# A chunk of scans waits for its own delta, B and C, and the parts of all images form one stream

## The chip, the cores and the metric

The kernel runs on one core of a Trainium2 chip. The metric is the device time of one execution in microseconds. Before the change three runs took 23043.62, 23055.54 and 23061.29 us; the median, 23055.54 us, is what the change is measured against.

A core has five engines that take their instructions in order, each from its own queue: TensorE (PE, with its weight loads shown as PEld), VectorE (DVE), ScalarE (ACT), GpSimd (POOL) and SyncE (SP), which here issues nearly all DMA transfers. They wait for each other through semaphores.

## The reference, cut to what matters

Eight images of 56 x 56 tokens and 192 channels go through four residual layers, each behind a group norm. The last layer is a selective state-space scan in four directions over the tokens:

```python
x = x + _L0_conv_ref(_gn(x), ...)   # gate over two Toeplitz products
x = x + _L1_conv_ref(_gn(x), ...)   # attention in shifted windows
x = x + _L2_conv_ref(_gn(x), ...)   # depthwise 3 x 3
x = x + _L3_conv_ref(_gn(x), ...)   # selective scan

def _selective_scan(u, delta, A, Bm, Cm, Dp, delta_bias):
    delta = jax.nn.softplus(delta + delta_bias[None, :, :, None])
    dA = jnp.exp(delta[:, :, :, None, :] * A[None, :, :, :, None])
    dBu = (delta * u)[:, :, :, None, :] * Bm[:, :, None, :, :]
    ...
    _, hs = jax.lax.associative_scan(comb, (dA, dBu), axis=-1)
    y = jnp.einsum('bkdnl,bknl->bkdl', hs, Cm)
    return y + Dp[None, :, :, None] * u
```

Here the scan has 384 channels (3 blocks of 128 partitions), 16 states a channel, 3136 tokens and 4 directions, for each of 8 images. `delta`, `Bm` and `Cm` come from the same image's tokens through small matrix products. All is fp32.

## The kernel before, in words

The first part computes the products q*v and the Toeplitz products of all images and leaves them in device memory. What follows concerns the rest, which works image by image.

**The front of an image** is a generator, `front(b)`: `gate`, `attention`, `conv2`, `inner`, `steps`, one after the other. They pass their results through device memory, and all carve their working space out of one SBUF tile, `slab`. A generator yields between small pieces of work, and tells at each yield how many PSUM banks it holds and needs, and whether a load must first land. `steps(b)` is the last stage and makes what the scans read. It has 14 parts, over `o` (0 for the row-wise directions, 1 for the column-wise ones) and `j` (seven chunks of 448 tokens). Each part makes B and C of its chunk (a product on PE, a copy at L853, a store to `bc_d`) and the deltas of two directions (products at L861, bias on ACT at L866, one softplus on ACT at L870 between two loads of function tables, two stores to `dl_d` at L873). All stores and loads here are issued on SP.

**The scans** go over 224 chunks (8 images x 4 directions, called slots, x 7 chunks), in each of which there are 24 "pairs" (3 channel blocks `d` x 8 pairs of states `k`), 5376 pairs in all, 672 an image. A pair is: inject on POOL (delta*u times B, L991), decay on ACT (two exponentials, L1006), one scan on DVE (L1015), the product with C (L1021, on POOL for three of eight `k`, on DVE for the others), the copy of the state for the next chunk (L1028, ACT), and adding up over the states on PE (L1036). Slots 0 and 1 read the `o` = 0 part of `steps`, slots 2 and 3 the `o` = 1 part. A chunk's delta is loaded by `load_delta`, its u by `load_xc`, B and C by `load_bc`, all one chunk ahead.

**The finish** of an image, `finish(b, j)`, normalises and projects one of seven chunks of the summed result. It runs during slot 0 of the next image.

**The order of the work** is made when the program is built. A loop over the pairs emits the scan's instructions, and after each pair calls `parts.step(limits)`. The clients of `parts` are generators, the front of the next image and the current `finish`. `step` goes through them, first those that hold a PSUM bank, and resumes one as long as a small model of each engine's due times says that its piece fits within the limits. Two loops call `step` with the limits `anything`, which means that whatever is left is emitted at once: one before the first chunk of the next image, until its front is done, and two before `ending`, the current `finish`, is wanted done. Since each engine works in the order of emission, everything so forced stands ahead of the next pairs of scans.

The front of image `b + 1` is added at the first pair of image `b`. The loop that forces it stands in the last chunk of image `b`, at (d, k) = (1, 0), which is the 16th pair from the end of the image:

```python
if i + 1 in range(4 * NCH, len(chunks), 4 * NCH):
    while fronts[b + 1] in parts.clients:
        parts.step(anything)
load_delta(i + 1)
```

For image 0 the front runs alone, ahead of the scans. In the last image no front runs.

Of the kernel before, what the change touches and what calls it, by code (L numbers as in the profile page):

```python
# [28 lines left out]
NCH = L // CH  # L29
# [52 lines left out]
def model(ctx: ExitStack, tc: tile.TileContext, a: dict, out: bass.AP):  # L82
    nc = tc.nc
    B = out.shape[0]
# [195 lines left out]
    with (  # L280
# [42 lines left out]
        def bank():  # L323
            return ps.tile([128, 512], F32, name="ps_f")
# [35 lines left out]


        meter, costs = Meter(tc.nc), {}


        st = wp.tile([CP, 2, NCH, 6], F32, name="gn_st")
# [466 lines left out]
        def steps(b):  # L832

            w_x, xc, rc, dl = carve(slab, 128, (2, ND, 128), (2, ND, CH), (2, CH), (2, ND, CH))
            nc.sync.dma_start(out=w_x, in_=a["w_x"])
            todo = [(o, j) for o in range(2) for j in range(NCH)]

            def load_x(n):
                o, j = todo[n]
                nc.sync.dma_start(out=xc[:, n % 2], in_=xc_d[o][b][:, :, j * CH : (j + 1) * CH])  # L840

            load_x(0)
            yield 0, 0, 8.0
            for n, (o, j) in enumerate(todo):
                tok = slice(j * CH, (j + 1) * CH)
                if n + 1 < len(todo):
                    load_x(n + 1)
                yield 0, 1
                p = bank()
                for d in range(ND):  # L850
                    nc.tensor.matmul(p[:, :CH], w_x[:, o, d, :], xc[:, n % 2, d, :], start=d == 0, stop=d == ND - 1)
                yield 1, 0
                nc.scalar.copy(rc[:, n % 2, :], p[:, :CH])  # L853
                nc.sync.dma_start(out=bc_d[o][b][:, tok], in_=rc[64:, n % 2, :])
                for d in range(ND):
                    yield 0, 2
                    held = []
                    for s in range(2):
                        row = slice(32 * s, 32 * s + R)
                        held.append(bank())  # L860
                        nc.tensor.matmul(  # L861
                            held[s][:, :CH], w_dt[row, o, d * 128 : (d + 1) * 128], rc[row, n % 2, :], start=True, stop=True
                        )
                    yield 2, 0
                    for s in range(2):
                        nc.scalar.activation(  # L866
                            dl[:, s, d, :], held[s][:, :CH], AF.Identity, bias=dt_b[:, 2 * o + s, d : d + 1]
                        )
                yield 0, 0
                nc.scalar.activation(dl, dl, AF.Softplus)  # L870
                usual_functions()
                for s in range(2):
                    nc.sync.dma_start(out=dl_d[2 * o + s][b][:, :, tok], in_=dl[:, s])  # L873
            yield 0, 0

        def front(b):
            yield from gate(b)
            yield from attention(b)
            yield from conv2(b)
            yield from inner(b)  # L880
            yield from steps(b)
# [171 lines left out]
        class Parts:  # L1053
# [36 lines left out]
                entry.held, entry.needs, *load = got  # L1090
                entry.ready = at + sum(load)

            def step(self, limit):
                old = [e for e in self.clients if e.held]
                for entry in old + [e for e in self.clients if e not in old]:
                    while entry in self.clients:
                        if entry.held and entry not in old:
                            break
                        if entry.needs + sum(e.held for e in self.clients if e is not entry) > 2:
                            break  # L1100
                        if not self.fits(entry, limit):
                            entry.waits += 1
                            break
                        entry.waits = 0
                        if entry in old:
                            old.remove(entry)
                        self.resume(entry)
# [27 lines left out]
        with tc.manual_schedule():  # L1135
            for k in range(NP):
                load_bc(0, k)
            load_delta(0)
            for d in range(ND):
                xcs[0, d] = load_xc(0, d)  # L1140
                times_x(0, d)
            ahead, last = 2, len(pairs) - 1
            parts = Parts()
            run = parts.run

            fed, set_, scanned, taken, summed = ([0.0] * (len(pairs) + ahead + 8) for _ in range(5))

            def feed(g):
                inject(g)
                fed[g] = run("P", 2.09, taken[g - 5] if g > 4 else 0.0)  # L1150

            def take(g):
                times_c(g)
                after = scanned[g], summed[g - 4] if g > 3 else 0.0
                taken[g] = run("P", 2.0, *after) if on_pool(*pairs[g][1:]) else run("D", 1.09, *after)

            def prepare(g):
                decay(g)
                set_[g] = run("A", 1.3, taken[g - 2] if not on_pool(*pairs[g - 2][1:]) else scanned[g - 2])

            for g in range(ahead):
                feed(g)
            initial(0), initial(1)
            prepare(0)
            fronts = {}
            ending, anything = None, dict.fromkeys("ADE", 1e9)
            for g, (i, d, k) in enumerate(pairs):
                b, slot, j = chunks[i]
                if i % (4 * NCH) == 0 and d == 0 and k == 0 and b + 1 < B:
                    fronts[b + 1] = parts.add(front(b + 1), "front")  # L1170
                more = i + 1 < len(chunks)
                if more and d == 1 and k == 0:
                    if i + 1 in range(4 * NCH, len(chunks), 4 * NCH):
                        while fronts[b + 1] in parts.clients:
                            parts.step(anything)
                    load_delta(i + 1)
                    for e in range(ND):
                        xcs[i + 1, e] = load_xc(i + 1, e)
                if more and (d, k) in ((1, 6), (1, 7), (2, 0)):
                    times_x(i + 1, d + k - 7 if d == 1 else 2)  # L1180
                    run("P", 1.08)
                pi, pd, pk = pairs[g - 1]
                if g + ahead <= last:
                    feed(g + ahead)
                if g and on_pool(pd, pk):
                    take(g - 1)
                if g:
                    keep_state(g - 1)
                    run("A", 0.15, scanned[g - 1])
                if g < last:  # L1190
                    prepare(g + 1)
                if g + 2 <= last:
                    initial(g + 2)
                    run("A", 0.12, taken[g - 3] if g > 2 else 0.0)
                scan(g)
                scanned[g] = run("D", 2.02, set_[g], fed[g])
                if not on_pool(d, k):
                    take(g)
                if g and pd == ND - 1 and pi + 1 < len(chunks):
                    load_bc(pi + 1, pk)  # L1200
                done = (i, d - 1) if d else (i - 1, ND - 1)
                if k == 2 and g > NP and chunks[done[0]][1] == 0:
                    xds[done] = load_xc(*done)
                if slot == 0 and b > 0 and (d, k) == (1, 4):
                    while ending.at < 3:
                        parts.step(anything)
                if k == 4 and g > NP:
                    sums(*done)
                if slot == 0 and b > 0 and ((j, d, k) == (0, 0, 5) or j + 1 < NCH and (d, k) == (2, 4)):
                    while ending in parts.clients:  # L1210
                        parts.step(anything)
                    ending = parts.add(finish(b - 1, j + (d == 2)), "finish")

                n1 = max(parts.t["D"], fed[g + 1], set_[g + 1])
                n2 = n1 + (2.02 if on_pool(*pairs[min(g + 1, last)][1:]) else 3.11)
                parts.step({"A": max(n2, fed[g + 2]) - 0.7, "E": n1 + 5.0, "D": 0.2})
                if g >= 2:
                    add_up(g - 2)
                    summed[g - 2] = run("E", 1.1, taken[g - 2])
            if on_pool(d, k):  # L1220
                times_c(last)
            for g in (last - 1, last):
                add_up(g)
            sums(i, d)
            for j in range(NCH):
                drain(finish(B - 1, j))
# [101 lines left out]
```

## Time and profile before

| | |
|---|---|
| median of three runs | 23055.54 us |
| profiled execution, as timed | 23085.27 us |
| its span, first to last instruction | 23083.3 us |
| mean granted TensorE clock | 0.887 |
| PE busy | 18554.5 us, 80% |
| DVE busy | 16579.4 us, 72% |
| POOL busy | 16157.3 us, 70% |
| ACT busy | 12534.0 us, 54% |
| first scan to end of the last | 3727.4 to 22874.9 us |

The shares are means over stretches of different kinds. The first 3.7 ms are the products, the Toeplitz part and the front of image 0. Then come eight images of scans, each about 2330 to 2490 us from its first scan to the next image's, the last one 2014 us. All scans together are 5376; a scan takes 2.02 us on DVE, an inject 2.10 us and a product with C 2.02 us on POOL, 1.09 us on DVE.

The profile has several views: a page with busy tenths in 40 slices, the waits (who waited for whom, the total, how often, the longest), the timeline of an engine, and busy times by stretch. In a stretch's line stand its bounds and length, for each engine its busy time and in brackets the number of its instructions, then the granted clock, the DMA share and the rate in GB/s.

### The profile page before, as it was taken

The numbers are of one execution on the slowest core, as the hardware profiler recorded it, in microseconds if no ns is written. First come the engines' busy times: TensorE is split into PE (matmuls) and PEld (weight loads), VectorE is DVE, ScalarE is ACT, GpSimd is POOL, SyncE is SP. The second block draws the span as 40 slices with busy tenths as digits, with TensorE's granted clock in tenths as the row PEclk, the third lists the DMA queues.
The fourth block names the chain that finished last, engine by engine and source line by source line (L and its number), as shares of the span: only waits on it lengthen the run. The fifth ranks groups of instructions, "written<-read, shape, count | busy, mean of one in ns | idle before, by whom it ended". The sixth has DMA issues, their size and how long they took to land. (4 is left out here: it accounts for less than half of the span.)

```text
span 23083.3 us, 201064 instructions
## 1 busy us (share of the span) xinstructions
PE 18554.5 (80%) x58660; PEld 9730.9 (42%) x58660; DVE 16579.4 (72%) x13156; ACT 12534.0 (54%) x31864; POOL 16157.3 (70%) x8500
## 2 busy tenths in 40 slices
PE   8866678888887878888888888887888798887666
PEld 4566334434443435343543444343434353333323
DVE  3211114997789768986899778976898689877996
ACT  3211225655666565756565566656664657565554
POOL 0000004987789768976898778877897689778997
PEclk9987778999899989998999889998999899988888
DMA  3488225445544455345544454345534553454332
GB/s 89 109 196 178 67 62 171 135 123 168 167 135 131 142 169 146 124 135 172 151 134 129 161 162 137 122 147 177 148 115 146 168 157 119 140 172 139 126 122 89
DMA packets 2536339, 3220.44 MB, mean 140 GB/s; under 512 B 1045261, under 2 KB 2488687, under 8 KB 2504272
## 3 DMA queue, kind: packets, MB, share of 16 engines
q1 hardware_dynamic: 2515010, 3091.32, 45.2%
q0 software_dynamic: 15520, 116.14, 1.3%
q8 instruction: 465, 7.62, 0.1%
q14 instruction: 640, 5.24, 0.1%
q10 hardware_dynamic: 4704, 0.12, 0.0%
HBM read 2631.56 MB, written 575.48 MB: 139 GB/s over the span
## 5 line engine op out<-in xcount | busy, mean ns | idle before, releaser
L991 POOL TENSOR_TENSOR hs<-du,bm 128x896 f32<-128x896 f32 x5376 | 11124.4, 2102 | 110.1 <-DVE ps_a L1015 90.2
L1036 PE MATMUL ps_y<-hc,ident_sb 128*128 128x448 f32 x21504 | 9913.8, 597 | 947.8 <-POOL hc L1021 846.4
L1015 DVE TENSOR_TENSOR_SCAN ps_a<-ps_a,hs 128x898 f32<-128x898 f32 x3360 | 6793.9, 2022 | 1048.5 <-ACT ps_a L1006 871.5
L1006 ACT ACTIVATE ps_a<-delta,A_logs_sb 128x449 f32<-128x449 f32 x10752 | 6859.4, 638 | 322.2 <-DVE hs L1015 35.9
L1036 PEld LDWEIGHTS ps_y<-hc,ident_sb 128*128 128x128 f32 x21504 | 4339.0, 210 | 5095.4 <-issue 3594.3
L1021 POOL TENSOR_TENSOR hc<-hs,cm 128x896 f32<-128x896 f32 x2016 | 4067.0, 2017 | 2757.2 <-DVE hs L1015 1574.0
L1015 DVE TENSOR_TENSOR_SCAN hs<-ps_a,hs 128x898 f32<-128x898 f32 x2016 | 4064.5, 2016 | 810.3 <-ACT ps_a L1006 779.3
L1021 DVE TENSOR_TENSOR hc<-ps_a,cm 128x896 f32<-128x896 f32 x3360 | 3668.9, 1092 | 1166.1 <-PE ps_y L1036 883.2
L1028 ACT COPY state<-ps_a 128x2 f32<-128x2 f32 x3359 | 528.6, 157 | 4109.0 <-DVE hc L1021 4106.4
L979 POOL TENSOR_TENSOR du<-delta,xcd 128x448 f32<-128x448 f32 x672 | 716.0, 1066 | 1266.1 <-DMA xcd<-xc 1266.1
L263 PE MATMUL ps_tz<-tzx,tm 112*112 112x112 f32 x4608 | 889.3, 369 | 463.5 <-issue 294.7
L802 PE MATMUL ps_f<-slab 128*128 128x448 f32 x2646 | 1096.9, 551 | 85.0 <-DMA slab<-dg_d 58.0
L277 POOL DMA_DIRECT2D o<-tzx x192 | 97.8, 513 | 1490.9 <-DVE tzx L269 1340.1
L263 PEld LDWEIGHTS ps_tz<-tzx,tm 112*112 112x112 f32 x4608 | 883.8, 199 | 469.2 <-issue 468.1
L269 DVE COPY tzx<-ps_tz 112x448 f32<-112x448 f32 x288 | 179.9, 625 | 1172.3 <-PE ps_tz L263 862.0
L996 ACT COPY hs<-state 128x2 f32<-128x2 f32 x4608 | 817.5, 177 | 2.7 <-POOL hc L1021 2.6
L76 PE MATMUL ps_f<-slab 96*96 96x448 f32 (+6 forms) x2306 | 745.3, 519 | 76.1 <-DMA slab<-x 37.4
L269 ACT COPY tzx<-ps_tz 112x448 f32<-112x448 f32 x288 | 153.2, 532 | 1198.1 <-PE ps_tz L263 1067.2
L632 PE MATMUL ps_f<-ident_sb,slab 98*98 98x98 f32 x1344 | 337.9, 322 | 576.3 <-ACT slab L625 576.3
L734 PE MATMUL ps_f<-slab 96*96 96x448 f32 x1764 | 728.9, 549 | 46.4 <-DVE slab L721 46.4
L802 PEld LDWEIGHTS ps_f<-slab 128*128 128x128 f32 x2646 | 509.4, 193 | 598.0 <-issue 528.7
L861 PE MATMUL ps_f<-slab,w_dt_sb 12*128 12x448 f32 x1176 | 507.5, 787 | 309.8 <-ACT slab L853 234.9
(215 smaller groups left out, 17788.8 us busy)
## 6 DMA issues: line engine op xcount, KB each, us to landing
bm<-bc SPq DMA_DIRECT2D x1792, 448.0 KB
cm<-bc SPq DMA_DIRECT2D x1792, 448.0 KB
xcd<-xc SPq DMA_DIRECT2D x840, 224.0 KB
dl<-slab SPq DMA_DIRECT2D x224, 672.0 KB
delta<-dl SPq DMA_DIRECT2D x224, 672.0 KB
tzx<-qv SPq DMA_DIRECT2D x192, 588.0 KB
o<-tzx POOLq DMA_DIRECT2D x192, 588.0 KB, 16.3
slab<-x SPq DMA_DIRECT2D x224, 336.0 KB
```

The costliest lines, as they stand in the source:

```text
L76: return f(*args, **kw)
L263: nc.tensor.matmul(po[:, c, :], t[:, c2 + c, :], x[:, :, c1 + c2 + c], start=True, stop=True)
L734: nc.tensor.matmul(p[:CP, :CH], dg[:, k, t, :], xp[:, u, k, dy : dy + 8, dx : dx + W], start=t == 0, stop=t == 8,)
L802: nc.tensor.matmul(p[:, :CH], dg[:, t, :], xp[:, 8 * j + dy : 8 * j + dy + 8, dx : dx + W], start=t == 0, stop=t == 8,)
L979: nc.gpsimd.tensor_mul(du[:, 0, :], deltas[i][:, d, 1 : CH + 1], xcs.pop((i, d)))
L991: nc.gpsimd.tensor_mul(hs[:, :, tokens(i)[0]], dus[i, d].to_broadcast([128, NG, CH]), bms[i, k])
L996: nc.scalar.copy(hss[g][:, :, tokens(i)[1]], src)
L1006: nc.scalar.activation(dA[:, n, :], deltas[i][:, d, at : at + CH + 1], AF.Exp, scale=negA[:, slot, d, c : c + 1])
L1015: nc.vector.tensor_tensor_scan(h, dA, hs, 0.0, ALU.mult, ALU.add)
L1021: (nc.gpsimd if on_pool(d, k) else nc.vector).tensor_mul(hc, h[:, :, tokens(i)[0]], cms[i, k])
L1028: nc.scalar.copy(states[i][:, d, NG * k : NG * k + NG], h[:, :, tokens(i)[2]])
L1036: nc.tensor.matmul(yps[i, d][:, :CH], ident, hcs[g][:, n, :], start=k + n == 0, stop=k + n == NP + NG - 2)
```

## The change

A set `made` now holds which parts (b, o, j) of `steps` have been emitted. Before a chunk's delta is loaded, the loop forces the front only until that chunk's own part is in the set; this test is made ahead of every chunk, not at the first chunk of an image alone. The front of the next image that has none is added as soon as the former one has ended, even if the scans of the current image are not yet at their start or are in their middle; there is at most one front at a time. `step` gets an argument `only`: when a client is to be forced, the others are resumed only while they hold a PSUM bank. All three forcing loops use it. No operation, no transfer and no buffer is added or taken away; the order of emission changes.

```diff
         meter, costs = Meter(tc.nc), {}
+        made = set()
...
                 for s in range(2):
                     nc.sync.dma_start(out=dl_d[2 * o + s][b][:, :, tok], in_=dl[:, s])
+                made.add((b, o, j))
             yield 0, 0
...
-            def step(self, limit):
+            def step(self, limit, only=None):
                 old = [e for e in self.clients if e.held]
                 for entry in old + [e for e in self.clients if e not in old]:
+                    if only is not None and entry is not only and not entry.held:
+                        continue
                     while entry in self.clients:
...
-            fronts = {}
+            ahead_of, b_next = None, 1
             ending, anything = None, dict.fromkeys("ADE", 1e9)
             for g, (i, d, k) in enumerate(pairs):
                 b, slot, j = chunks[i]
-                if i % (4 * NCH) == 0 and d == 0 and k == 0 and b + 1 < B:
-                    fronts[b + 1] = parts.add(front(b + 1), "front")
+                if ahead_of not in parts.clients and b_next < B:
+                    ahead_of = parts.add(front(b_next), "front")
+                    b_next += 1
                 more = i + 1 < len(chunks)
                 if more and d == 1 and k == 0:
-                    if i + 1 in range(4 * NCH, len(chunks), 4 * NCH):
-                        while fronts[b + 1] in parts.clients:
-                            parts.step(anything)
+                    b1, slot1, j1 = chunks[i + 1]
+                    while (b1, slot1 // 2, j1) not in made:
+                        parts.step(anything, ahead_of)
                     load_delta(i + 1)
...
                 if slot == 0 and b > 0 and (d, k) == (1, 4):
                     while ending.at < 3:
-                        parts.step(anything)
+                        parts.step(anything, ending)
...
                     while ending in parts.clients:
-                        parts.step(anything)
+                        parts.step(anything, ending)
                     ending = parts.add(finish(b - 1, j + (d == 2)), "finish")
```

## The prediction

> **What bounds the kernel now.** I read the page first: its slices, then the groups of the scan. The chain of waits that ended last covers the final image alone and says nothing of the places that the change touches, so after the page I went to the waits of all engines, to the boundaries in time, and to the rate of the scan by stage.
>
> ```profile
> DVE  3211114997789768986899778976898689877996
> POOL 0000004987789768976898778877897689778997
> ```
>
> The scans begin in the seventh slice (first scan at 3727 us) and end at 22875 us. In this stretch no engine is full, except POOL in the last image, where no front runs beside the scans. So the stretch is a mixture, and I look for what stops the scans:
>
> ```profile
> POOL hc L1021 <- DVE hs L1015: 1574.0, 513, 82.4
> DVE ps_a L1015 <- ACT ps_a L1006: 871.5, 295, 344.4
> DVE hs L1015 <- ACT ps_a L1006: 779.3, 106, 81.0
> ```
>
> Columns: total us, times, longest. The longest waits (some 80 us) are out of all proportion to a scan of 2.02 us. The timeline of VectorE and of ScalarE at one of them, at the end of the fourth image (the bracket is idle time and what ended it):
>
> ```profile
> 13361.48 2.04 DVE L1015 TENSOR_TENSOR_SCAN ps_a<-ps_a,hs 128x898 f32<-128x898 f32 x1 [3.37 <-ACT ps_a L1006]
> 13363.62 1.09 DVE L1021 TENSOR_TENSOR hc<-ps_a,cm 128x896 f32<-128x896 f32 x1
> 13439.82 2.03 DVE L1015 TENSOR_TENSOR_SCAN hs<-ps_a,hs 128x898 f32<-128x898 f32 x1 [75.11 <-ACT ps_a L1006]
> ```
> ```profile
> 13434.46 2.44 ACT L870 ACTIVATE slab<-slab 128x2688 f32<-128x2688 f32 x1
> 13436.92 1.28 ACT L321 ACT_TABLE_LOAD   x1
> 13438.21 0.16 ACT L1028 COPY state<-ps_a 128x2 f32<-128x2 f32 x1
> 13438.41 1.31 ACT L1006 ACTIVATE ps_a<-delta,A_logs_sb 128x449 f32<-128x449 f32 x2
> ```
>
> The scan waits for its decay factors (L1006), which stand on ScalarE behind the rest of `steps` of the next image: the planner's loop emitted all of it there. All engines, in three of the seven such stretches, and the sum over all seven (busy us and instructions of PE, PEld, DVE, ACT, POOL, then clock and DMA):
>
> ```profile
> 5959.80:6017.30 57.50, 44.59 (x76) 15.98 (x74) 1.13 (x2) 36.49 (x42) 3.24 (x2) 0.64 0.33 114
> 8421.30:8503.40 82.10, 61.12 (x96) 21.77 (x96) 1.09 (x1) 49.41 (x57) 1.84 (x1) 0.63 0.39 132
> 13363.60:13439.80 76.20, 61.41 (x92) 22.03 (x92) 1.09 (x1) 46.25 (x54) 0.00 (x0) 0.58 0.37 126
> ...
> sum 520.50, PE 408.49 PEld 146.16 DVE 7.68 ACT 316.92 POOL 5.07; mean PE 58.36 PEld 20.88 DVE 1.10 ACT 45.27 POOL 0.72
> ```
>
> POOL, the fullest engine of the scans, does 5 us of work in 520 us. Last, scans per stretch (busy us of L1015 and its count). Fourth image: gate with `finish` beside it, free `steps`, the forced stretch, the tail. Then the first image's gate, without `finish`; then the last image, without a front, its first 153 pairs with `finish`, the rest without:
>
> ```profile
> 11013.00:11554.00 541.00, 279.96 (x139) 0.95 0.55 152
> ...
> 13148.00:13361.00 213.00, 118.48 (x59) 0.83 0.58 204
> 13361.00:13439.00 78.00, 2.04 (x1) 0.58 0.38 130
> 13439.00:13481.00 42.00, 29.94 (x15) 0.85 0.49 160
> ```
> ```profile
> 3730.00:4161.00 431.00, 261.50 (x130) 0.96 0.58 161
> ```
> ```profile
> 20861.00:21369.00 508.00, 307.37 (x153) 0.86 0.43 139
> 21369.00:22872.00 1503.00, 1038.95 (x518) 0.86 0.37 122
> ```
>
> Length over count is the price of a pair: gate and finish 541/139 = 3.89 us, steps 213/59 = 3.61, tail 42/15 = 2.80, gate alone 431/130 = 3.32, finish alone 508/153 = 3.32, nothing beside 1503/518 = 2.90.
>
> **What the Trainium skill says.** "TensorE: Matmul & The Clock Gate", specification table, gives ScalarE, VectorE and GpSimdE a strict first-in first-out queue. The trace agrees: L1006 starts 0.2 us behind the last `steps` instruction, though its inputs had long been there. "ScalarE: Activation LUTs", section "What ACT_TABLE_LOAD costs", says that each load of a table takes about 1283 ns; the trace has 1.28 us, two for each part of `steps`, forced or not, so the change saves none of them. Part 1 of the first page says that an idle PE is clocked down; the granted clock of 0.58 to 0.64 in the forced stretches agrees, and there PE sets no pace.
>
> **The change part by part.** Counts are from the order in which both programs are built; it holds no times. A pair is one scan.
>
> Removed: in before, the last parts of `steps` are forced at pair 656 of each image: 303 of 7 x 128 pieces (a piece runs from one yield to the next), some 45 per image. The scan-to-scan times there are 59.5, 84.2, 78.3, 78.3, 78.3, 78.4 and 78.1 us, 535 in all. Seven ordinary pairs at 3.1 would be 22: gross gain 513 us.
>
> Given back: the same pieces now run beside scans. In before 83 free pieces took 59 pairs, so 45 need some 32. In the built order the front covers the tails (16 pairs of each image) and then runs on into the next: `steps` ends 4, 16, 32, 44, 58, 67 and 67 pairs past the image's end, the next gate begins one pair later. So 110 tail pairs go from 2.80 to 3.61: +89. The lag only shifts later fronts until the last image, where 63 pairs that had only `finish` beside them get `steps` too. This sum, `steps` with `finish`, occurs nowhere in the trace. Adding the surcharge of `finish` (3.32 - 2.90 = 0.42) to 3.61 gives 4.03, so 63 x 0.71 = +45. In the earlier images `steps` takes the gate's place beside `finish`, and the gate comes out at the other end: by the same adding this cancels, since the gate falls from 3.89 to 3.32 outside `finish`. Together +134.
>
> The unknown is thus the price of 260 pairs with both. Lower bound 3.61 (finish hides wholly behind what steps waits for): 260 x 0.42 = 109 better. Upper bound: a surcharge of 1.0, the dearest that the trace has (by the starts of the scans, attention's 81 pairs beside finish take 4.17 us, its others 3.14; the change of stage is in it): 260 x 0.58 = 150 worse. I take 0.42, because the surcharge seen with the gate (0.57, a start of 13 us in 139 pairs among it) is near it.
>
> Still forced: the built order has 7 pieces of the sixth `steps` and, at the seventh, 9 pieces of the end of `inner` and 11 of `steps`, since a lag of 67 pairs leaves the first part too late. A forced piece costs 76.2/45 = 1.7 us: 27 x 1.7 = +46. Bounds: 20 (part of it hidden by scans already fed) and 90 (the seventh crosses from `inner` to `steps`, whose first load must land; that crossing shows scan-to-scan times of 10 to 13 us in the free case).
>
> Gate right behind `steps`: w_p, w_o, x and the o blocks now stand on SP behind the last two delta stores; the first o block overlays those deltas in the slab and must wait for the landing. In the forced stretch a ScalarE instruction waited for such a store until some 5 us after its issue (issued from 13405.89 to 13407.09, the wait over at 13412.07). Behind on SP stand bm, cm, delta and xcd of the next chunk, wanted 5 or more pairs (15 us) later: cost 0, at worst 5 us x 6. The absorb at L396 waited 10 us for w_p before (59.4 us in six) and will again; if w_p comes 5 us later, 30 more. I take 0, with 0 to 60 for the range.
>
> The delta, B and C loads behind the new wait: where the part is made in good time, the store is tens of pairs old and nothing waits. The two waits for `ending` alone: `finish` ends before its boundary in every image of before and is forced for 3 pieces in after, so nothing.
>
> Sum: -513 + 134 + 46 = -333 us on a span of 23083 us, to 22750. The profiled run took 23085.3, 30 us above the median of 23055.5. So 22722 us is the forecast against the median, 1.4% faster.
>
> **The rivals.** Crowding: `finish`, `steps` and two scans' decay contend on ScalarE and PE at the image's start, the 260 pairs cost the upper bound, and the clock, 0.83 in the steps stretch, falls further now that PE has no pause. For it: PE is 79% busy in that stretch (167.9 of 213 us). Against: the planner counts ScalarE and PE before it lets a piece in. Then -333 + 150 + 30 = -153: 22900.
>
> More gain: `finish` hides behind `steps`, and the forced pieces cost little: -333 - 109 - 20 = -462: 22594.
>
> Slower: the handover on SP. The gate's loads stand in front of the B and C loads, wait for landing delta stores, and POOL's inject (in order, L991) starves, and all scans behind it. It decides from 333/7 = 48 us per handover on; at 80 us it is +227: 23280. Against: 5 us is what a landing costs, a tenth of that.
>
> No effect: the stall comes back as forced pieces. The order shows 27 for 303, so this would need the trace to price them ten times dearer: about 23055.
>
> **How the numbers follow.** Chances: forecast 0.74, crowding 0.12, more gain 0.07, no effect 0.03, slower 0.04. The range must hold 0.8: the forecast's own bounds (-109-26-0 to +150+44+60, not all at once) and part of both neighbours give 22605 to 22870. A change under 0.2% (46 us) can't be told from none. Faster 0.93, same 0.03, slower 0.04.
>
> **What would show it.** Scan-to-scan times near 78 us gone at pair 656 of the first five images; some 12 us at the sixth and 35 at the seventh. Steps with finish near 4.0 us a pair. Tails near 3.6 rather than 2.8. Front work until about 67 pairs into the last image. It is wrong if POOL shows new waits for bm at the handovers, or pairs at the image's start cost 4.6 or more.

## The result and the profile after

The changed kernel takes 22642.83 us (median of four runs, 22639.56 to 22648.44) against 23049.58 us before on the same chip; the ratio is 0.9826, with a 95% interval of 0.9809 to 0.9843. That is 407 us less; 333 were forecast, and 22643 lies in the range. Run again later beside two variants on another chip, it had a ratio of 0.9819 (0.9806 to 0.9833). The chips differ by some 50 us in the kernel before, so I compare ratios below, or kernels of one chip, or traces (whose scans took 18708.7 and 18739.7 us for this one kernel on the two chips).

The profiled execution went from a span of 23083.3 us to 22646.7 us. Nothing of the 436.6 us is outside the scans: from the first scan's start to the last one's end it was 19147.5 us and is 18708.7 us, 438.8 less.

First the waits of VectorE in the changed kernel (total, times, longest; L1015 is now L1017, L1006 is L1008):

```profile
DVE ps_a L1017 <- ACT ps_a L1008: 875.2, 317, 345.2
DVE hc L1023 <- PE ps_y L1038: 830.4, 580, 9.5
...
DVE hs L1017 <- ACT ps_a L1008: 279.7, 93, 43.7
```

The last line is the one that held the stops. It had 779.3 us with a longest wait of 81.0. The first line hardly moved (871.5 before); its longest wait, 344 or 345 us, is the one ahead of the first scan, whose factors come from the first image's front. I had shown it as evidence of the stops, which it is not.

Then pair 656 of each image, where before all engines stood behind the forced part of `steps`. The fourth, sixth and seventh of the seven stretches (from the end of one scan to the start of the next; busy us and instructions of PE, PEld, DVE, ACT, POOL, then clock and DMA):

```profile
13144.40:13145.40 1.00, 1.00 (x4) 0.49 (x3) 0.98 (x1) 0.99 (x2) 1.00 (x1) 1.00 0.00 0
...
17907.50:17919.10 11.60, 7.24 (x17) 2.42 (x15) 1.12 (x2) 9.40 (x13) 0.00 (x0) 0.74 0.15 55
20287.80:20332.60 44.80, 14.38 (x24) 5.59 (x24) 1.09 (x1) 23.48 (x27) 2.33 (x2) 0.58 0.43 163
```

Scan to scan the seven are now 3.1, 6.0, 3.1, 3.1, 3.1, 13.7 and 46.9 us, where they were 59.5 to 84.2. The two that are left are the sixth and seventh, in which the built order still forces 7 and 20 pieces.

And the scans (L1017) by stretch: `steps` without `finish` and with it at the fourth image's end and the fifth one's start, `steps` with `finish` in the last image, and the last image's rest; then the tail of the fourth image, the 15 pairs behind its pair 656:

```profile
13047.00:13196.00 149.00, 86.25 (x43) 0.83 0.59 202
13215.00:13370.00 155.00, 80.73 (x40) 0.90 0.60 197
...
20404.00:20644.00 240.00, 127.26 (x63) 0.90 0.57 192
20932.00:22436.00 1504.00, 1039.25 (x518) 0.87 0.37 122
```
```profile
13145.40:13196.70 51.30, 30.05 (x15) 0.86 0.59 200
```

That is 3.47, 3.88, 3.81 and 2.90 us a pair, and 3.42 in the tail, which took 2.80 before. Over all seven fronts `steps` costs some 3.6 without `finish` and 3.9 with it.

Adding up the time from each scan's start to the next by the stage of the front that the built order has there gives the whole account (the stops are the scans that took over 30 us):

| stage of the front | before: pairs, us | after: pairs, us | difference, us |
|---|---|---|---|
| stops | 7, 535 | 1, 47 | -488 |
| none | 778, 2308 | 605, 1798 | -510 |
| steps | 419, 1512 | 621, 2321 | +809 |
| gate | 967, 3684 | 952, 3578 | -106 |
| attention | 1820, 5802 | 1815, 5753 | -49 |
| conv2 | 434, 1699 | 434, 1691 | -8 |
| inner | 951, 3609 | 948, 3521 | -88 |

The first three rows are what the change moves. The last three are stages in which it changes nothing, and they became cheaper by 145 us. For `attention` this is only the company that it keeps: 81 of its pairs stood in the first 153 pairs of an image, beside `finish`, at 4.17 us, and now 11 do; elsewhere it cost 3.14 before and 3.17 after. `inner` is another matter. It has the same 213 pieces a front in both kernels, beside nearly the same number of pairs, never beside `finish`, and took 3.795 us a pair before and 3.714 after. Here it is in the third image, before (L1015) and after (L1017), where it begins 19 pairs later:

```profile
10163.50:10680.90 517.40, 273.92 (x136) 0.92 0.47 153
```
```profile
10112.20:10604.40 492.20, 271.66 (x135) 0.94 0.48 157
```

This was not foreseen, and the second half of the experiments is about it.

### The profile page after: what moved, and what is told of

It reads as the page before. It is cut to its first block, busy times and chain, and to the rows that moved or that the text cites. A ratio compares the mean times of both kernels' runs of the same rounds, so it can differ in the third digit from the quotient of the medians.

```text
span 22646.7 us, 201012 instructions
## 1 busy us (share of the span) xinstructions
PE 18356.6 (81%) x58660; PEld 9667.8 (43%) x58660; DVE 16589.1 (73%) x13156; ACT 12505.2 (55%) x31864; POOL 16161.0 (71%) x8500
## 5 line engine op out<-in xcount | busy, mean ns | idle before, releaser
L1017 DVE TENSOR_TENSOR_SCAN ps_a<-ps_a,hs 128x898 f32<-128x898 f32 x3360 | 6795.2, 2022 | 1083.2 <-ACT ps_a L1008 875.2
L1008 ACT ACTIVATE ps_a<-delta,A_logs_sb 128x449 f32<-128x449 f32 x10752 | 6860.0, 638 | 332.3 <-DVE hs L1017 47.3
L1017 DVE TENSOR_TENSOR_SCAN hs<-ps_a,hs 128x898 f32<-128x898 f32 x2016 | 4063.9, 2016 | 348.9 <-ACT ps_a L1008 279.7
L618 ACT ACTIVATE slab<-slab,mxs 98x98 f32<-98x98 f32 x1344 | 489.5, 365 | 360.8 <-DVE mxs L615 360.8
```

Source lines behind the costliest of these rows:

```text
L1008: nc.scalar.activation(dA[:, n, :], deltas[i][:, d, at : at + CH + 1], AF.Exp, scale=negA[:, slot, d, c : c + 1])
L1017: nc.vector.tensor_tensor_scan(h, dA, hs, 0.0, ALU.mult, ALU.add)
```

## The experiments

All variants are made from the changed kernel. "Forced" counts the pieces of a front that a forcing loop emits, from the built order: 303 before, 27 in the changed kernel. "Start" is the pair of its image at which a front starts: 0 each time before; 0, 5, 17, 33, 45, 59 and 68 in the changed kernel, because each front starts one pair behind the end of the former one.

One thing needed no run. A kernel in which a front may not start ahead of its image builds to the same order of instructions on all five engines as the changed one. The fronts end late, 4 to 67 pairs into the next image, and none ever starts early; so that a front may start ahead of its image gives nothing here. It acts only where fronts end ahead of their image, as next.

**How much is forced.** Two kernels ask for more of `steps` before an image's first chunk, all 14 parts (e1) and 11 (e2):

```diff
-                    while (b1, slot1 // 2, j1) not in made:
+                    last_part = (b1, 1, NCH - 1) if i + 1 in range(4 * NCH, len(chunks), 4 * NCH) else (b1, slot1 // 2, j1)
+                    while last_part not in made:
```

> The changed kernel, but the first chunk of an image waits for all 14 parts of steps as before; the next gate still comes right behind. By the built order 152 pieces are forced (303 before the change, 27 after it). Main theory, the gain is the forced pieces alone: a forced piece costs 76.2/45 = 1.7 us and would have cost 0.5 us beside the scans (0.71 pairs of 0.72 us more), so 1.2 us net; 125 more pieces than the changed kernel give +150 us on 22643, that is 22793, with stops of some 34 us (20 pieces) at pair 656 of the images. Rival, it is the wait for a chunk's own part that matters, whatever is forced: back to within 50 us of 23050.

Measured: ratio 0.9862 (0.9847 to 0.9877), 22784 us. That it meets the 22793 of the forecast is a matter of the chip: the forecast starts from 22643 us, and on e1's chip two kernels that equal the changed one (e3 and e5, below) took 22674 and 22680. So the 125 pieces cost 104 to 110 us, not 150: some 0.85 us each net, not 1.2.

> The same with 11 of the 14 parts asked for at the first chunk. 119 pieces are forced. Main theory: 92 more than the changed kernel at 1.2 us, +110 us, 22753; with e1 and the two kernels a straight line of time over forced pieces. Rival as in e1: above 22950.

Measured (the second has `(b1, 1, 3)` for `(b1, 1, NCH - 1)`): ratio 0.9921 (0.9906 to 0.9935), 22919 us. Two stops of each, at the third and fourth image's end, in the same columns as above:

```profile
10828.80:10865.50 36.70, 25.49 (x43) 8.84 (x41) 1.09 (x1) 23.83 (x28) 2.68 (x2) 0.64 0.34 118
13243.80:13279.60 35.80, 25.40 (x40) 8.54 (x38) 1.10 (x2) 23.17 (x27) 3.40 (x2) 0.62 0.35 121
```
```profile
10838.80:10874.20 35.40, 24.41 (x42) 8.74 (x40) 1.09 (x1) 22.10 (x27) 1.91 (x1) 0.70 0.41 141
13275.60:13311.00 35.40, 24.93 (x36) 8.66 (x36) 1.12 (x2) 22.08 (x27) 1.83 (x1) 0.56 0.41 141
```

The price of a forced piece at the stop holds: 20 pieces stop the scans for 38.8 us scan to scan, 19 for 37.5, so 1.8 us each beyond an ordinary pair, where 1.7 was taken. The rival (any wait for whole `steps` brings it all back) is out: with it, e1 keeps 1.4 of the 1.8%. There the second half of the change does act: the gate starts 15 pairs before the image, so 20 pieces are left to force instead of 45.

But the straight line of time over forced pieces is out as well. e2 forces fewer pieces than e1 (119, 152), stops no longer, and is 0.6% slower. Forced pieces explain the stops, not the rest. e1's fronts start at pair -15, e2's at pair 1.

**The handover on SP, and `only`.** One kernel (e3) moves the deltas and rc (the copies of B and C) within the slab, so that the gate's first o block no longer overlays deltas on their way out; another (e5) leaves out the argument `only` in the three forcing loops.

```diff
-            w_x, xc, rc, dl = carve(slab, 128, (2, ND, 128), (2, ND, CH), (2, CH), (2, ND, CH))
+            w_x, xc, _, dl, _, rc = carve(
+                slab, 128, (2, ND, 128), (2, ND, CH), (640,), (2, ND, CH), (2368,), (2, CH)
+            )
```

> The changed kernel with another layout of the slab in steps: the deltas lie where the gate's s comes to lie and rc lies at the slab's end, so that the gate's first load of o overlays no delta that is still being stored. Main theory, the handover on SP costs little: 22643 within 20 us. Rival, the held SP queue delays B, C and w_p at each of six handovers: 60 us or more are gained.

Measured: 0.9814 (0.9799 to 0.9828); scans 18725.5 us in the trace, against 18708.7 of the changed kernel.

```diff
-                        parts.step(anything, ahead_of)
+                        parts.step(anything)
...
-                        parts.step(anything, ending)
+                        parts.step(anything)
```

> The changed kernel without the argument only: a forcing loop drives all clients again. By the built order 31 front pieces are forced instead of 27. Main theory: 4 pieces at 1.2 us, 22648 within 20 us. Rival, holding the others back carries part of the gain: 22690 or more.

Measured: 0.9819 (0.9803 to 0.9836); scans 18726.1 us. Both are the changed kernel's time within what can be told. What the overlay costs stands in the changed kernel's waits: SP holds the gate's o load (L430) until a delta store has landed, and POOL's inject waits for a late B. In e3 SP has no wait for a delta store.

```profile
SPq L430 <- DMA dl<-slab: 9.5, 6, 4.1
```
```profile
POOL hs L993 <- DMA bm<-bc: 4.6, 3, 2.5
```

SP's longest total wait, for the buffer of bm, is the same with and without the overlay (first the changed kernel, then e3):

```profile
SPq L966 <- POOL hs L993: 3662.7, 203, 53.7
```
```profile
SPq L968 <- POOL hs L995: 3662.5, 200, 53.2
```

So the handover costs nothing that shows, and `only` carries none of the gain.

**The gate's due time.** In the changed kernel VectorE still idles at the start of six fronts until the gate's weights w_p have landed, which its first VectorE work, the absorb (L397), scales. This kernel (e6) changes `yield 0, 0, 6.0` in the gate, the time that the planner allows for the load, to 16.0.

> The changed kernel with a due time of 16 us instead of 6 for the gate's first loads, so that the absorb (L397) is emitted when w_p has landed. In the changed kernel DVE idles 65.4 us in six such waits. Main theory: these waits stop the scans at the handover, and some 50 us go (ratio to before 0.9804 where the changed kernel has 0.9826). Rival, the stop is filled later by pairs that run ahead, or returns as lag: 0 within 15 us.

Measured: 0.9821 (0.9807 to 0.9834). The waits of VectorE for w_p, changed kernel and e6:

```profile
DVE slab L397 <- DMA slab<-in_w_p_dram: 65.4, 6, 13.4
```
```profile
DVE slab L397 <- DMA slab<-in_w_p_dram: 66.6, 6, 13.9
```

The edit doesn't do what it should: the idle time is still there. The built order shows why. In both kernels the absorb of these six fronts is emitted in the same pair as the loads. A new front's due time starts from `ready`, which is 0.0, on a clock that runs from the first pair; so the first loads count as landed at 6 or 16 us of the whole run, which is long past when the second front starts. Only the first front, which starts at 0, obeys: its absorb comes two pairs after the loads instead of one. What a gate without this wait would gain stays open.

**Where a front stands.** To get rid of the last forced pieces I widened the planner's limit for PE from n1 + 5.0 to n1 + 6.5 (e7), where n1 is the time at which its model can start the next scan.

```diff
-                parts.step({"A": max(n2, fed[g + 2]) - 0.7, "E": n1 + 5.0, "D": 0.2})
+                parts.step({"A": max(n2, fed[g + 2]) - 0.7, "E": n1 + 6.5, "D": 0.2})
```

> The changed kernel with the planner's limit for PE at n1 + 6.5 instead of n1 + 5.0. By the built order no piece at all is forced, and the front ends within 7 pairs of each image's end, so that hardly any front work stands in the last image. Main theory: the forced stops left at the sixth and seventh image (46.9 us and some 20) and 60 pairs with a front in the last image at some 0.6 us go: -85 us, ratio 0.979. Rival, crowding: PE works longer ahead of the scans' adding up, and pairs beside a front get dearer by 2% or more: +80 us, ratio 0.986.

Measured: 0.9915 (0.9901 to 0.9928), 200 us slower than the changed kernel, with no forced piece and no stop left. It looks like crowding by the wider limit. The next kernel (e8) has the same limit and holds each front until pair 8:

```diff
-                if ahead_of not in parts.clients and b_next < B:
+                if ahead_of not in parts.clients and b_next < B and g >= 4 * NCH * ND * NP * (b_next - 1) + 8:
```

> e7 with the next front held until the eighth pair of an image: again nothing is forced, the fronts start at pairs 8 to 11 of an image where e7 has -6 to 5. Theory after e1 and e2 (equal stops, 136 us apart): it counts where in the image the front starts against finish, so more than 40 us from e7, slower. Rival, the start's place is nothing: within 15 us of e7.

Measured: 0.9842 (0.9828 to 0.9855). The hold alone, which delays the fronts by 6 to 14 pairs, gives 172 us. The expectation had the place count, but made the later start the slower one; its sign was wrong. A further kernel (e9) joined e6 and e7:

> e6 and e7 together; nothing is forced. If their effects are of different places they add up: some 50 us under e7, ratio 0.977. If the due time only moves the stop, equal to e7 within 15 us.

Measured: 0.9910 (0.9896 to 0.9923), as e7, since the due time again acts on the first front alone (idle time 59.0 us). Two more limits are to separate limit and place (e10 and e11):

> The changed kernel with the planner's PE limit at n1 + 5.5 (5.0 there, 6.5 in e7). By the built order nothing is forced and the fronts start at pairs 0, 3, 16, 25, 39, 45 and 51 of their images, much as in the changed kernel (0, 5, 17, 33, 45, 59, 68). Theory that a front's place against the chunks sets the price: 40 to 60 us under the changed kernel, from its stops of 46.9 and some 20 us, ratio 0.980. Rival, it was the wider limit that made e7 dear: a third of e7's loss of 200 us less the stops, some 20 us or more over the changed kernel.

Measured: 0.9798 (0.9785 to 0.9811), 22640 us.

> The same at n1 + 5.75. Nothing is forced, but now the fronts start at pairs 0, -5, 3, 6, 6, 6 and 6, as in e7. Theory of the place: 25 to 36 us an image over five images dearer than e10, that is 125 to 180 us, ratio near 0.987. Rival, the limit alone: halfway between the changed kernel and e7 in proportion, 1/6 of the way from e10, 30 us over e10.

Measured: 0.9917 (0.9903 to 0.9931), 22913 us, 273 more than e10, where the place was to cost 125 to 180 and the limit 30. Beside them on the same chip (e12):

> The changed kernel once more, beside e10 and e11 on one chip: ratio 0.9826 within 0.0017, as first measured. Should it be off by more, then ratios of different chips can't be compared to 0.2%, and the comparisons rest on the traces' scan stretches.

Measured: 0.9819, 22682 us; first and second measurement agree. A quarter of a microsecond in the limit costs 273 us, while a step twice as wide, from 5.0 to 5.5, gains 42. So the cost isn't in proportion to the limit. But e10 and e11 differ in limit and order at once, and don't show that the limit has no cost of its own; only e8 against e7 moves the order alone. What changes with the limit is the whole order, and in it the fronts' starts (0, 3, 16, 25, 39, 45, 51 in e10; 0, -5, 3, 6, 6, 6, 6 in e11). The fifth to the seventh image as a whole, first in e10 and then in e11 (columns as for the stops):

```profile
13210.00:15606.00 2396.00, 2023.25 (x6378) 1019.18 (x6377) 2013.45 (x1546) 1487.22 (x3851) 2002.45 (x1036) 0.91 0.49 149
15606.00:17977.00 2371.00, 2010.09 (x6395) 1012.28 (x6394) 2006.97 (x1547) 1491.68 (x3856) 2004.64 (x1037) 0.93 0.50 151
17977.00:20345.00 2368.00, 2006.90 (x6415) 1011.65 (x6413) 2015.66 (x1547) 1500.37 (x3863) 2009.74 (x1039) 0.93 0.49 152
```
```profile
13353.00:15796.00 2443.00, 2050.57 (x6411) 1025.02 (x6411) 2023.56 (x1547) 1502.57 (x3865) 2004.33 (x1036) 0.91 0.48 147
15796.00:18237.00 2441.00, 2040.55 (x6412) 1021.92 (x6412) 2024.97 (x1547) 1503.20 (x3867) 2006.42 (x1038) 0.91 0.48 147
18237.00:20667.00 2430.00, 2039.00 (x6415) 1021.78 (x6414) 2022.61 (x1547) 1503.68 (x3867) 2003.57 (x1036) 0.91 0.48 148
```

The work is the same (the counts of every engine agree within 1% and POOL's busy time within 0.4%), neither has a stop, and an image takes 47 to 70 us longer in e11. In the first of the three the granted clock is the same. The waits of VectorE for PE to free the buffer of the product with C, in e10 and in e11:

```profile
DVE hc L1023 <- PE ps_y L1038: 868.1, 584, 10.6
```
```profile
DVE hc L1023 <- PE ps_y L1038: 1026.6, 631, 10.1
```

POOL's wait for the same buffers went from 619.7 to 810.7 us. So in the dearer order PE's adding up is late more often, and PE is also slower: in the last of the three, where the counts of matmuls agree, it has 32 us more busy time, at a granted clock of 0.91 where e10 has 0.93.

Adding up by stage, as in the table above, shows where the orders differ. Beside `finish` means here in the first 153 pairs of an image:

| kernel | scans, us | attention pairs beside `finish` | `steps` pairs beside `finish` | `inner`, us a pair |
|---|---|---|---|---|
| before | 19147.5 | 81 | 0 | 3.80 |
| changed | 18708.7 | 11 | 295 | 3.71 |
| e7 | 18974.4 | 77 | 22 | 3.78 |
| e8 | 18786.4 | 30 | 66 | 3.78 |
| e10 | 18690.3 | 11 | 236 | 3.73 |
| e11 | 18974.1 | 69 | 33 | 3.79 |

Where a front starts decides which of its stages meets `finish`. Beside `finish` a pair with `steps` costs some 0.25 us more than elsewhere (3.87 against 3.62 in the changed kernel), with no front 0.49 (3.39 against 2.90), with the gate 0.56 (3.92 against 3.36), with attention 1.03 (4.17 against 3.14 before). By these prices the exchange makes some 90 of e11's 284 us over e10 in the traces, an estimate. `inner` makes another 50; the rest lies mostly in dearer pairs of `steps` and of the gate.

If the start alone set an image's price, all fronts at e10's cheapest place should be better still. The last kernel (e13) has the limit n1 + 5.55 and a hold until pair 44:

> The changed kernel with the PE limit at n1 + 5.55 and the next front held until pair 44 of its image. By the built order the fronts start at pairs 44, 49, 51, 51, 51, 51 and 51, and no front piece is forced. Theory of the place: e10's image whose front starts at 51 takes 2367 us, its images 1 to 6 2392 in the mean; all at 51 gives 6 x 22 us less, some 130 us under e10, ratio 0.974. Rival, e10's last images were cheap by other causes, and the 44 pairs held in image 0 and the lag of 50 pairs in the last image only cost: within 40 us of e10, or above it.

Measured: 0.9786 (0.9772 to 0.9799), 22584 us. It is the fastest of all, but by 41 us in the traces' scans (18649.1 against e10's 18690.3), not by 130. Images with a front at 49 or 51 took 2375 to 2393 us where e10's took 2367. The intervals of e10 and e13 overlap, so the ratios alone don't tell them apart, and 41 us is little more than the 31 between the two traces of the changed kernel. The theory has the sign right at most, and the price isn't a function of the start alone. In this order no attention pair stands beside `finish`, 355 `steps` pairs do, and `inner` costs 3.67 us a pair, the least of all.

## Why the prediction was right, and where its sum was off

**The stops.** Right in place, cause and size: -513 + 46 forecast, and the 535 us of the seven pairs 656 have become 79 (46.9 at the seventh image, 13.7 at the sixth, five between 3.1 and 6.0), which is -456. The forced pieces were priced at 1.7 us and cost 1.8 in e1 and e2. The forecast of 12 and 35 us for the two that remain measured 10.6 and 43.8 above an ordinary pair; the crossing from `inner` to `steps` is in the larger one.

**What is given back.** The tails, 15 pairs of each image, went from 291 to 366 us, +75 where +89 was forecast (3.49 us a pair and not 3.61). The 63 pairs of the last image cost 3.81 (4.03 forecast), so the surcharge of `finish` on `steps` was mis-sized: some 0.3 over all fronts where 0.42 was taken. The last image as a whole grew by 38.5 us, 45 forecast.

**The step that failed** is "by the same adding this cancels", the nothing put down for the images ahead of the last. These three terms make -342 in the trace. It lost 438.8, and the missing 97 us lie elsewhere. In the first 153 pairs of the second to seventh image, beside `finish`, the exchange does cancel: 3590.5 us before, 3593.3 after. It is outside them, ahead of pair 656, that 12717.2 us became 12617.8. By its own prices the prediction's sum there wasn't nothing: a pair of gate with `finish` and one of `steps`, 3.89 + 3.61, became 4.03 + 3.32, which is 0.15 less, or 30 us for 197 pairs. In the trace 204 pairs of `steps` outside `finish` gave way to 142 of the gate and 65 of attention, which at the prices of before is -72. `inner`, which the prediction left as it was, gave -76; attention became dearer by 42 and the rest by 8. The first is thus a sum that was mis-sized; the cause of the second is open.

That a shift of the fronts alone can be worth this much, e8 against e7 shows: 172 us at one limit, with no piece forced in either. e11 against e10 is 273 us, with the limit in it. So the term that stood at nothing can be of this size, with either sign. That it fell on the good side was luck as far as the forecast goes, which had bounds for `steps` with `finish`, but none for this.

**The rivals.** Crowding by 260 dear pairs did not come: 3.92 a pair against the 4.6 it needed. The handover on SP cost nothing that shows (e3): six waits for a landing store make 9.5 us, and POOL waited for bm 4.6 us in all, in three waits. The seven stops did not come back as forced pieces.

**What stays open** is most of why the place of a front matters. Which stage meets `finish` is a part of it; that `inner`, the gate and `steps` get dearer by themselves is not accounted for. The traces show PE late and PE slower in the dear orders; whether the clock falls because PE pauses longer between better packed bursts, or PE is late because the clock is lower, or a third thing (long ScalarE pieces meeting the sums at a chunk's end) drives both, no run here tells apart. Nor does one hold the order and move the limit. A rule "start at pair 51" doesn't hold up: e13 got a third of what it promised.

## What to carry to other kernels

Where a planner forces what is left at a boundary, look for the stop in the timeline at that boundary and price a forced piece there; asking only for the part that the next step reads takes the stop away. Beside the scans the same work cost a third of what it cost alone: 878 free pieces of `steps` made 621 pairs dearer by 0.84 us each (2321 us, at 2.90 without a front 1801), 0.6 us a piece against 1.8, with the surcharge of `finish` in it. When such a change shifts one stream against another, list which stages meet before and after and price each meeting, and put a term of both signs for the rest into the sum: here a shift was worth more than half a per cent with nothing forced and nothing added. A knob that seems to do nothing may not be connected: e6's due time was counted from the wrong zero. And tell a limit's own effect from the order that it makes, by moving the order alone, before calling a wider limit too wide.

## What was not expected of the hardware

Nothing in a single instruction. In the streams together: 58660 matmuls of the same shapes took 18435.9 us of PE's busy time in e11 and 18287.3 us in e10, 0.8% apart on one chip, at a mean granted clock of 0.890 and 0.898. Busy time times clock is 16408 and 16422 us, 16429 in the changed kernel and 16458 before. So the lower clock accounts for PE's longer work, and what lowers it is the question. The clock went roughly with the time through the kernels (0.887 before, 0.895 after, 0.900 in e13). In the stops it was 0.56 to 0.74, but stops don't set the mean alone: e1 has seven and 0.895, e11 has none and 0.890. Nor was PE at rest in the stops: in the one at 13363.60 us before it was busy 61.41 of 76.20 us, with no pause over 2.3 us, at a clock of 0.58.
